# Two stores at the end of a kernel, each issued as two halves on two DMA queues

## The chip, the cores and the metric

The kernel runs on one core of a Trainium2 chip. The core has a matrix engine (TensorE, PE in the profile), VectorE (DVE), ScalarE (ACT), GpSimd (POOL) and SyncE (SP). Transfers between the core's on-chip memory (SBUF) and the device's memory run on 16 DMA engines. An instruction on an engine's own queue issues a transfer; in this kernel SyncE, ScalarE and GpSimd issue them. A store's completion is counted in a semaphore, and the program ends when all stores are complete.

The metric is the device time of one execution, in microseconds (us). Three runs of the kernel before took 293.83, 294.07 and 294.32 us; the median is 294.07.

## What is computed

The input `x` has 8 batches of 1024 tokens with 512 features in float32; `cond` is one row of 512 per batch. Cut to what matters, the reference is:

```
for every batch b:
    ae    = layernorm(cond[b]) * ln_g + ln_b
    h     = gelu(ae @ w1 + b1)
    xw    = h @ w2 + b2                          # two halves, each [512, 8]
    layer = base_layer + x_a @ x_b.T             # a term of rank 8 for every batch
    y     = x + (x + x @ layer)                  # 2x + x @ layer
    ys    = cond[b] / sqrt(512)
    d     = rsqrt((ys*ys) @ (weight*weight) + 1e-8)
    out[b] = y + ((y * ys) @ weight) * d
```

For each batch the two layers fold into one matrix of 512 by 512, so that `out[b] = x[b] @ M[b]`. Making the eight matrices takes the first part of the kernel; multiplying 1024 token rows by each fills the rest. To keep float32 accuracy each operand of a product is split into a rounded part and a remainder, and three matmuls are added up (rounded by rounded, and the two cross terms).

## The kernel before

**The main loop** (`main`) takes batches 0 to 4 and half of batch 5 in tiles of 128 tokens. TensorE accumulates 12 matmuls per tile in PSUM, ScalarE copies the result to SBUF and issues its store on its own queue, 256 KB at a time. SyncE loads `x` in blocks of 512 tokens (1 MB), and the splitting and the making of later matrices run beside it.

**The end of the kernel** is the class `Seven`. For the second half of batch 5 and for batches 6 and 7 it multiplies blocks of 512 tokens by 512 columns with seven products of half size instead of eight, in Strassen's manner. One call of `part` does one such block of 512 tokens. The seven products come in the order of `Seven.ORDER`: 1, 5, 6, 2, 7, 3, 4. Every product has 12 matmuls, six for each of two row groups of 128 tokens (`m` is 0 or 1). The last product of the last part is therefore number 4, and its result is the lower left quarter of the block: 256 tokens by 256 columns.

Output tiles are `o1` (the upper 256 tokens) and `o2` (the lower 256 tokens), each of 128 partitions, two row groups and 512 columns. After a product, ScalarE copies a PSUM bank into a quarter of such a tile, or VectorE adds a bank onto it (line 1032).

**The last call**, `s7.part(1, last=True)` (line 1128), differs in two ways from the others. The bank that products 6, 7 and 4 share is two tiles, one per row group (line 1020), so that the first row group can be copied while TensorE works on the second. And every quarter is stored by itself: the store of products 2, 7 and 3 is issued by SyncE, that of product 4 by ScalarE, row group by row group (lines 1035 and 1036). So after the last matmul of the first row group ScalarE copies it (A, 128 tokens by 256 columns, 128 KB), issues its store, copies the second row group (B, likewise) and issues that store.

**What sets the order.** Matmuls always keep the order in which the program writes them. `ve`, `se` and `sy` are wrappers of VectorE, ScalarE and SyncE; while `InOrder.on` is true, what is issued through them keeps the written order too, and it is set to true before the parts begin (line 1120). So in the stretch around the change every instruction stands on its engine in the order of the code. Waits between engines come from semaphores, which the framework derives from the parts of tiles that are read and written. Stores and loads on SyncE's and ScalarE's queues take eight semaphores in rotation. At the end SyncE waits for all of them, before the engines meet at closing barriers.

Of the kernel before, what the change touches and what calls it, by code (L numbers as in the profile page):

```python
# [14 lines left out]
P = 128  # L15
# [15 lines left out]
def cond_resid_kernel(ctx: ExitStack, tc: tile.TileContext, small, cond, condrows, consts,  # L31
# [32 lines left out]
    ve, se, sy = InOrder(nc.vector), InOrder(nc.scalar), InOrder(nc.sync)  # L64
# [333 lines left out]
    rows = ppool.tile([P, KC, D], F32, tag="ph", name="rows")  # L398
# [506 lines left out]
    class Seven:  # L905
# [99 lines left out]
        def part(self, g, steps=(), last=False, then=None):  # L1005


            b, bank, steps = self.b, {}, iter(steps)
            o1, o2 = (pools["late"].tile([P, 2, D], F32, tag="o2", name=f"o{i}_{b}_{g}", bufs=4)
                      for i in range(2))  # L1010
            for p in self.ORDER:
                key = {5: "z", 3: "z", 2: "v"}.get(p, "w")

                def new(key, count=1):
                    pool, tag = (po, "po") if key == "z" else (acc, "acc")
                    bank[key] = [pool.tile([P, 2, HD], F32, tag=tag, name=f"s{key}{i}_{b}_{g}")
                                 for i in range(count)]

                if p in (1, 5):
                    new(key, 2 if p == 1 and last else 1)  # L1020
                self.product(g, p, bank[key], p in (1, 5))
                if p == 1:
                    new("v")
                o, cols = {1: (None, None), 2: (o1, slice(0, HD)), 3: (o1, slice(HD, D)),
                           6: (o1, slice(HD, D)), 4: (o2, slice(0, HD)), 5: (o2, slice(HD, D)),
                           7: (o2, slice(HD, D))}[p]
                for m, u in enumerate(bank[key]):
                    u, to = (u, slice(0, 2)) if len(bank[key]) == 1 else (u[:, 0:1], slice(m, m + 1))
                    if p == 1:
                        se.copy(bank["v"][0][:, to], u)  # L1030
                    elif p in (3, 7):
                        ve.tensor_add(o[:, to, cols], u, o[:, to, cols])
                    else:
                        se.copy(o[:, to, cols], u)
                    if last and p in (2, 3, 7, 4):
                        self.store(se if p == 4 else sy, o, g, int(p in (4, 7)), to, cols)
                    elif p in (3, 4):
                        self.store(sy, o, g, int(p == 4), to, slice(0, D))
                next(steps, None)
                if p == 7 and then:  # L1040
                    then()

        def store(self, queue, o, g, half, ms, cols):
            at = g * HT + 2 * P * half
            queue.dma_start(
                out[self.b, at + P * ms.start:at + P * ms.stop, cols].rearrange("(m p) d -> p m d", p=P),
                o[:, ms, cols])

    def late_pools():
        making.close()  # L1050
# [147 lines left out]
```

## Time and profile before

| | |
|---|---|
| median of three runs | 294.07 us |
| the profiled execution | 293.74 us |
| its span in the profile | 291.9 us |
| TensorE busy | 286.3 us (98%) |
| VectorE, ScalarE busy | 214.8 us (74%), 175.0 us (60%) |
| granted clock of TensorE | 0.998 on average |
| last PSUM copy by ScalarE (B) | starts 288.52, takes 0.37 us |
| last store issued (B) | at 288.93 us, 0.34 us at the issue |

The profile is of one execution. Busy times are sums over the span; times of instructions count from the span's start. A name such as `ACTq` stands for the queue side of an engine: instructions that issue transfers or handle semaphores, which are not counted as busy. "Landing" is the time from the issue of a transfer to its completion. In a table by stretches the columns are the stretch, its length and TensorE's busy time with its count of instructions, then the same for weight loads, VectorE, ScalarE and GpSimd, then the granted clock, the share of the 16 DMA engines that was busy, and GB/s. Nearly every line shows `L62` or `L45`, the wrappers through which the instructions go; tiles and times tell them apart.

### The profile page before, as it was taken

The page shows a single profiled execution, that of the slowest core. Times are in us where ns is not written, and L with a number is a line of the kernel's source. Part 1 is how long each engine was busy: PE and PEld are TensorE (multiplying, and loading weights), DVE is VectorE, ACT ScalarE, POOL GpSimd, SP SyncE. Part 2 cuts the span into 40 slices and gives each one's busy share as a digit, 9 for nine tenths or more (in the row PEclk, how much of TensorE's full clock was granted, in tenths as well). Part 3 has the DMA queues.
Part 4 walks back from the last instruction along what each step waited for, and adds up shares of the span by engine and source line. Part 5 has one row for each costly group of instructions (what it writes and reads, how often), then busy time and mean ns, then how long its engine had stood idle before and what let it go on. Part 6 is the DMA issues. An engine that isn't in the chain of part 4 may idle for free.

```text
span 291.9 us, 4100 instructions
## 1 busy us (share of the span) xinstructions
PE 286.3 (98%) x1519; PEld 225.2 (77%) x1519; DVE 214.8 (74%) x295; ACT 175.0 (60%) x272; POOL 35.9 (12%) x77
## 2 busy tenths in 40 slices
PE   7999999999999999999999999999999999999995
PEld 3665566467877878888877888887888889999994
DVE  2889898989916999519799565326789977798912
ACT  5757263286849884658654575544658745856641
POOL 2111000202944560000022000000000000000000
PEclk9999999999999999999999999999999999999999
DMA  7999999992799783332328114262175870852334
GB/s 209 405 429 413 411 403 405 390 383 90 187 321 322 235 250 116 110 145 93 159 80 263 55 72 135 83 216 74 72 251 176 291 257 1 290 204 87 142 146 144
DMA packets 19924, 62.14 MB, mean 213 GB/s; under 512 B 2736, under 2 KB 4016, under 8 KB 15552
## 3 DMA queue, kind: packets, MB, share of 16 engines
q1 hardware_dynamic: 9504, 43.76, 40.7%
q10 hardware_dynamic: 6912, 12.32, 11.5%
q0 software_dynamic: 3488, 5.79, 7.5%
q8 instruction: 12, 0.20, 0.3%
q14 instruction: 8, 0.07, 0.1%
HBM read 44.02 MB, written 17.84 MB: 212 GB/s over the span
## 4 chain that ended last, share of the span: by engine, by line
PE 96%; DMA 2%; ACT 0%; DVE 0%; SPq 0%; ACTq 0%; issue 0%
PE po L45 42%; PE pp L45 20%; PE sw L45 9%; PE px L45 5%; PE sz L45 5%; PE pg L45 4%; PE pq L45 4%; PE sv L45 2%; DMA b_raw<-in_baseT 2%; PE pr L45 1%; PE pt_t L45 1%; PE ps_t L45 0%; PE pq_v L45 0%; PE pq_z L45 0%; ACT o L62 0%; DVE o L62 0%
## 5 line engine op out<-in xcount | busy, mean ns | idle before, releaser
L45 PE MATMUL po<-ph,xs 128*128 128x512 f32 x352 | 113.7, 392 | 0.0
L45 PEld LDWEIGHTS po<-ph,xs 128*128 128x128 f32 x352 | 66.0, 188 | 15.6 <-issue 1.7
L45 PE MATMUL po<-pl,xs 128*128 128x512 f32 x176 | 68.6, 390 | 0.0
L62 ACT COPY o<-po 128x512 f32<-128x512 f32 x44 | 25.9, 588 | 35.0 <-PE po L45 35.0
L45 PEld LDWEIGHTS po<-pl,xs 128*128 128x128 f32 x176 | 33.0, 188 | 6.7
L62 DVE TENSOR_TENSOR xs<-x,xs 128x1024 fp32r<-128x1024 f32 (+1 forms) x23 | 27.0, 1176 | 15.0 <-ACT xs L62 15.0
L62 DVE TENSOR_TENSOR nl_p<-n,nh_p 128x1024 fp32r<-128x1024 f32 x21 | 25.7, 1222 | 12.4 <-ACT nh_p L62 12.4
L62 ACT CAST nh_p<-n 128x1024 fp32r<-128x1024 f32 x21 | 22.1, 1054 | 14.6 <-DVE n L62 10.9
L62 ACT CAST xs<-x 128x1024 fp32r<-128x1024 f32 x22 | 23.0, 1056 | 3.6 <-DMA x<-in_x 3.6
L62 ACT COPY q<-pp 128x512 f32<-128x512 f32 x30 | 17.4, 586 | 8.7 <-PE pp L45 8.6
L542 POOL DMA_DIRECT2D fa<-kept_a x28 | 13.8, 508 | 58.3 <-PE pr L45 54.0
L45 PE MATMUL pp<-nh_p,sh 128*128 128x512 f32 x48 | 19.0, 396 | 0.0
L45 PE MATMUL pp<-nh_p,sl 128*128 128x512 f32 x48 | 18.7, 390 | 0.0
L45 PE MATMUL pp<-nl_p,sh 128*128 128x512 f32 x48 | 18.7, 390 | 0.0
L62 DVE SCALAR_TENSOR_TENSOR n<-w_sb,ysT,d 128x512 f32<-128x512 f32 x24 | 16.9, 748 | 0.9 <-DMA d<-d_out 0.9
L62 ACT CAST sh<-sraw 128x1024 fp32r<-128x1024 f32 (+1 forms) x14 | 12.9, 926 | 6.8 <-DVE sraw L62 6.8
L62 DVE TENSOR_TENSOR sl<-sraw,sh 128x1024 fp32r<-128x1024 f32 (+1 forms) x14 | 14.9, 1067 | 2.2 <-ACT sh L62 2.2
L62 DVE TENSOR_TENSOR pl<-q,ph 128x1024 fp32r<-128x1024 f32 (+1 forms) x10 | 11.1, 1116 | 6.9 <-ACT ph L62 6.9
L45 PE MATMUL px<-w,hT 128*32 128x512 f32 x128 | 15.6, 599 | 0.0
L62 ACT COPY o<-sw 128x512 f32<-128x512 f32 (+1 forms) x12 | 6.2, 518 | 15.4 <-PE sw L45 12.3
L62 DVE TENSOR_TENSOR q<-pr,q 128x512 f32<-128x512 f32 x14 | 8.8, 688 | 7.9 <-PE pr L45 7.8
L62 DVE TENSOR_TENSOR n<-n,n 128x1024 f32<-128x1024 f32 x12 | 14.5, 1225 | 0.1
(199 smaller groups left out, 576.6 us busy)
## 6 DMA issues: line engine op xcount, KB each, us to landing
w<-in_w SPq DMA_DIRECT2D x16, 1024.0 KB, 10.4
x<-in_x SPq DMA_DIRECT2D x16, 1024.0 KB, 5.6
out<-o ACTq DMA_DIRECT2D x44, 256.0 KB, 2.3
out<-o SPq DMA_DIRECT2D x8, 512.0 KB, 2.9
fa<-kept_a POOLq DMA_DIRECT2D x28, 64.0 KB, 2.7
ft<-kept_t POOLq DMA_DIRECT2D x28, 64.0 KB, 3.5
d<-d_out POOLq DMA_DIRECT2D x6, 256.0 KB, 7.3
w_sb<-in_w SPq DMA_DIRECT2D x1, 1024.0 KB, 8.5
```

Of the source, the lines that this page charges most:

```text
L45: tc.keep_in_program_order(nc.tensor.matmul(*args, **kw))
L62: return lambda *a, **kw: pin(f(*a, **kw)) if InOrder.on else f(*a, **kw)
L542: nc.gpsimd.dma_start(fold[name, b][32 * c:32 * c + 32, :], kept[name, g][32 * i:32 * i + 32, :])
```

## The change

The store of product 4 in the last call of `part` is issued as two transfers per row group. Rows (partitions) 0 to 63 go by ScalarE's queue, and rows 64 to 127 by SyncE's, in that order in the program. `store` gets an argument for the rows, which is all 128 in every other use. All other stores keep their queue, size and place: products 2, 3 and 7 of the last part still go by SyncE. After A's copy there are now one issue on ScalarE and one on SyncE, and the same after B's copy; the bytes stored are the same.

```diff
-                    if last and p in (2, 3, 7, 4):
-                        self.store(se if p == 4 else sy, o, g, int(p in (4, 7)), to, cols)
+                    if last and p == 4:
+                        for queue, rows in ((se, slice(0, P // 2)), (sy, slice(P // 2, P))):
+                            self.store(queue, o, g, 1, to, cols, rows)
+                    elif last and p in (2, 3, 7):
+                        self.store(sy, o, g, int(p == 7), to, cols)
                     elif p in (3, 4):
                         self.store(sy, o, g, int(p == 4), to, slice(0, D))
...
-        def store(self, queue, o, g, half, ms, cols):
+        def store(self, queue, o, g, half, ms, cols, rows=slice(0, P)):
             at = g * HT + 2 * P * half
             queue.dma_start(
-                out[self.b, at + P * ms.start:at + P * ms.stop, cols].rearrange("(m p) d -> p m d", p=P),
-                o[:, ms, cols])
+                out[self.b, at + P * ms.start:at + P * ms.stop, cols].rearrange(
+                    "(m p) d -> p m d", p=P)[rows],
+                o[rows, ms, cols])
```

## The prediction

> **What bounds the kernel now.** I read the page first (engines, queues, the chain that ended last), then the end of the chain in order of time, the instructions of ScalarE and SyncE in the last microseconds, and the DMA engines' share in short stretches there.
>
> From the page, the engines' busy time and the chain by engine:
>
> ```profile
> PE 286.3 (98%) x1519; PEld 225.2 (77%) x1519; DVE 214.8 (74%) x295; ACT 175.0 (60%) x272; POOL 35.9 (12%) x77
> ...
> PE 96%; DMA 2%; ACT 0%; DVE 0%; SPq 0%; ACTq 0%; issue 0%
> ```
>
> TensorE carries the kernel, and the change touches none of its work. It can only act on what follows the last matmul. The end of the chain (start us, us, what):
>
> ```profile
> 286.97 0.70 DVE o L62
> 287.67 0.02 issue
> 287.69 0.38 ACT o L62
> 288.07 0.02 issue
> 288.09 0.34 ACTq L62
> 288.43 0.04 issue
> 288.47 0.02 ACTq L62
> 288.48 0.04 issue
> 288.52 0.37 ACT o L62
> ```
>
> ScalarE copies the first 128 token rows of product 4 out of PSUM (I call them A), issues their store, copies the second 128 rows (B) and issues theirs. The instructions show both issues, and SyncE's last one (the store of product 3):
>
> ```profile
> 288.09 0.34 ACTq L62 DMA_DIRECT2D out<-o  x1
> 288.52 0.37 ACT L62 COPY o<-sw 128x256 f32<-128x256 f32 x1 [0.46 <-PE sw L45]
> 288.93 0.34 ACTq L62 DMA_DIRECT2D out<-o  x1
> ...
> 287.69 0.38 SPq L62 DMA_DIRECT2D out<-o  x1
> ```
>
> Then the DMA engines in stretches (the last two columns are DMA share and GB/s):
>
> ```profile
> 288.00:288.50 0.50, 0.36 (x4) 0.16 (x2) 0.00 (x0) 0.06 (x1) 0.00 (x0) 1.00 0.00 0
> 288.50:289.00 0.50, 0.00 (x0) 0.00 (x0) 0.00 (x0) 0.37 (x1) 0.00 (x0) 1.00 0.80 270
> 289.00:289.30 0.30, 0.00 (x0) 0.00 (x0) 0.00 (x0) 0.00 (x0) 0.00 (x0) 1.00 1.05 352
> 289.30:289.70 0.40, 0.00 (x0) 0.00 (x0) 0.00 (x0) 0.00 (x0) 0.00 (x0) 1.00 1.04 336
> 289.70:289.80 0.10, 0.00 (x0) 0.00 (x0) 0.00 (x0) 0.00 (x0) 0.00 (x0) 1.00 0.62 205
> 289.80:290.20 0.40, 0.00 (x0) 0.00 (x0) 0.00 (x0) 0.00 (x0) 0.00 (x0) 1.00 0.92 312
> 290.20:290.40 0.20, 0.00 (x0) 0.00 (x0) 0.00 (x0) 0.00 (x0) 0.00 (x0) 1.00 0.08 21
> 290.40:291.90 1.50, 0.00 (x0) 0.00 (x0) 0.00 (x0) 0.00 (x0) 0.00 (x0) 0.62 0.00 0
> ```
>
> All 16 engines are full from 288.6 to 290.2 but for a dip at 289.7. Packet by packet the trace has product 3's 256 KB until 289.42, A's 128 KB from 289.32 to 289.77, and B's from 289.77 to 290.3. B's first packet comes 0.85 us after its issue, as product 3's does (287.69 to 288.55). So B starts when its issue allows, just as A's packets run out: issue delay and full engines meet there. B's last completion is recorded at 290.65, 1.73 us after its issue; another 1.28 us of closing waits and barriers end the span. The profiled execution took 293.74 us for a span of 291.93, 0.33 below the median of the three runs, 294.07; I work out the difference in its trace and add it to the median.
>
> **The change part by part.**
>
> ScalarE's issues: two before, two after, for half the rows. The 44 stores of 256 KB in the main loop took 338 to 351 ns each at the issue and these two of 128 KB 338, so length does not show in it; I take 338 again, 0. The other end: A's issue holds ScalarE until 288.43, and B's matmuls had released the copy at 288.38, so it starts some 0.145 late. An issue that shrank could win that much; one that grew to the longest such row on ScalarE, 414 ns at the start beside another queue's issue, would cost 2 x 0.08 = 0.15. What is queued behind A's issue is only B's copy and B's issue.
>
> SyncE's issues: two are added, at 344 to 345 ns by its own 128 KB stores at 285.31 and 286.05. A's half waits for the copy that ends at 288.06 and for SyncE itself, busy with product 3's issue until 288.07; with a wait on an older store's semaphore (17 ns, 0.05 to start) it goes out near 288.18. That is 0.09 behind ScalarE's half, and hidden: the engines are full with product 3 until 289.42, and 288.18 + 0.85 is 289.03. If that cover were gone, 0.09 would show. B's half waits for the second copy, whose end is signalled at 288.90; SyncE answered VectorE's signal of 287.668 at 287.685, so 288.92, level with ScalarE's 288.93. The old signals it also waits for are stores that landed by 281.8. Behind it on SyncE stand only the closing waits, which wait until 290.2 anyway. POOL's queue issues nothing in this stretch. Together 0.
>
> The data: each store still moves 128 packets of 1 KB, 8 per engine at 48 ns, 0.39 us. No row has stores of 64 rows or two queues that issue halves of one tile, so I bound it. Gain: a 256 KB store alone landed after 2.02 us, the 128 KB one after 1.73, so 128 KB less is 0.29 and 64 KB less 0.15, if the halves did not share engines; a share of 0.92 to 1.04 speaks against that. Loss: where the end of one 512 KB store met the start of the next (279.5 to 279.7), 2 KB packets took up to 131 ns instead of 85, a factor of 1.5; on the 16 packets per engine of A and B that is 16 x 48 x 0.5 = 0.39. I take 0, since queues seem to share engines without loss: A on ScalarE's queue followed product 3 on SyncE's at full rate. A store on ScalarE's queue also simply takes its turn behind SyncE's transfer. An x load issued at 178.07 and a store at 178.70 landed together (KB, us to landing), while a store with nothing before it took 2.0:
>
> ```profile
> x<-in_x SPq DMA_DIRECT2D x1, 1024.0 KB, 5.3
> out<-o ACTq DMA_DIRECT2D x1, 256.0 KB, 5.3
> ...
> out<-o ACTq DMA_DIRECT2D x1, 256.0 KB, 2.0
> ```
>
> The Trainium skill speaks against the change on "DMA: Bandwidth & Descriptors", section "Rules for kernel authors": two transfers of disjoint partition halves share the same 16 engines, and one transfer of 128 partitions is to be preferred. By it the data's term is 0 at best. A second page goes further: "SBUF — State Buffer", section "Door 1: The DMA port swizzle", says that partitions 0 to 63 reach 8 of the 16 ports; with the 27.2 GB/s per port that it works with, a half served by itself would run at 218 GB/s, and by my estimate from that page A and B would end 0.43 later. No row of the trace shows a half.
>
> Completions: every store ends with one 4-byte packet on each engine, 9 ns. Two more stores add 2 x 9 ns, 0.02 us.
>
> The closing waits: SyncE goes through the eight semaphores of the stores one after the other, each 0.061 us after the last (290.67, 290.73, ... 291.04). The stores take these eight in rotation; B has the second in that order, so six waits, long satisfied, are still gone through after B has landed. With two more stores in the rotation, A takes the first and second and B the third and fourth; four are left. That is 2 x 0.061 = 0.12 less. Its other end is 0, if the rotation restarts or the order changes.
>
> Sum: 0 + 0 + 0 + 0.02 - 0.12 = -0.10 us; 293.64 against the profiled 293.74, and 293.97 as a median. A kernel like this tells about 0.2%, 0.59 us, from no change, so I forecast no change.
>
> **The rivals.**
>
> The halves slow the packets. For it: nothing here has shown the engines serving half the rows. Against: equal bytes in equal packets. At the factor of 1.5 it gives -0.10 + 0.39, 294.36, still no change. If packets took twice as long, 16 x 48 = 0.77 more, 294.74. It decides from 0.69 us of loss on, that is 91 ns per packet.
>
> A wait takes the place of the copy's freedom (the other side). Four transfers now read two parts of one tile, on two queues. If the row halves made the dependency tracking take A's stores for readers of what the B copy writes, that copy would wait for A's landing: from 288.52 to 290.24 = 1.72 later, 294.07 + 1.72 - 0.10 = 295.69. It decides at once, since any wait on a store's landing is over 0.59. Against it: before, the B copy starts 0.43 us after A's issue, without waiting for its landing, and so did VectorE's second addition at 285.60, 0.29 us after the store of the first (landed 1.97 us after issue); both differ in columns of the tile that stay disjoint.
>
> The halves really help. Overlapping transfers (-0.15) and a shorter issue on ScalarE (-0.145) with the closing waits (-0.12): -0.42 at best, 293.65, still no change; it decides only if more of the landing time went away. Against: full engines, and an issue that was the same for 256 and 128 KB.
>
> The change does nothing at all (rotation not as I read it): +0.02, 294.09.
>
> **How the numbers follow.** The forecast, with or without the closing waits' 0.12: 0.60, of it 0.57 within 0.2%, 0.01 faster and 0.02 slower. Slower packets: 0.18, of it 0.07 within and 0.11 slower, because the price is unmeasured and the doubled one is past the bound. The wait on A's landing: 0.07, slower. The halves help: 0.11, of it 0.06 within and 0.05 faster, since the 0.35 from the last packet to the last completion may shrink too. Something unseen: 0.02 faster, 0.02 slower. Sum: faster 0.08, same 0.70, slower 0.22. The range takes the gain's end with the spread of the runs below the median, 293.65 - 0.15, about 293.5, and above the doubled packets' 294.74 and 0.15 for the spread, 294.9. It leaves out the wait on a landing. The likeliest case's own range is 293.7 to 294.3.
>
> **What would show it.** Right: four issues after 288, two on each queue, B's two level within 0.05; packets of 1 KB still near 48 ns; the last completion within 0.1 of 1.73 after issue; four satisfied waits after it instead of six, the time from the last landing to the span's end near 1.16 instead of 1.28. Wrong: packets over 60 ns or a DMA share of 1 that reaches past 290.4; a gap before the B copy; ScalarE's issue clearly off 338 ns; SyncE's half of B out after 289.

## The result and the profile after

The changed kernel took 294.57 us (median of 11 runs, 294.31 to 294.87), the kernel before 293.86 (11 runs, 293.75 to 294.32). The two medians are 0.71 us apart. The ratio that was recorded from the fast runs is 1.0019 with a 95% interval of 1.0012 to 1.0027: slower by 0.56 us, 0.35 to 0.79. The profiled execution has a span of 292.53 us against 291.93, 0.60 more. So it is a small loss. It is just under the 0.59 us that I had called the limit of what a measurement of this kernel tells, but the interval excludes no change.

TensorE's row is what it was, and so is the chain by engine:

```profile
PE 286.4 (98%) x1519; PEld 225.3 (77%) x1519; DVE 214.8 (73%) x295; ACT 175.0 (60%) x272; POOL 36.4 (12%) x77
...
PE 96%; DMA 1%; ACT 0%; DVE 0%; ACTq 0%; SPq 0%; issue 0%
```

The loss stands in the end of the chain (start us, us, what):

```profile
287.65 0.38 ACT o L62
288.03 0.02 issue
288.05 0.56 ACTq L62
288.61 0.04 issue
288.65 0.02 ACTq L62
288.67 0.04 issue
288.71 0.37 ACT o L62
```

The issue of A's first half holds ScalarE for 0.56 us; before, the issue of all of A took 0.34. The copy of B starts at 288.71, although TensorE had finished B's matmuls at 288.34. The second pair of issues, as the instructions of ScalarE and the rows of the stores show them (duration min/median/max in ns, then first and last start):

```profile
288.71 0.37 ACT L62 COPY o<-sw 128x256 f32<-128x256 f32 x1 [0.69 <-PE sw L45]
289.11 0.50 ACTq L62 DMA_DIRECT2D out<-o  x1
...
L62 SPq DMA_DIRECT2D out<-o x1: 467/467/467, 289.1 to 289.1; - x1
L62 ACTq DMA_DIRECT2D out<-o x1: 498/498/498, 289.1 to 289.1; - x1
```

Both queues issue B's halves at the same moment, as the change means them to, but each for 0.47 to 0.50 us. What the DMA engines did (last two columns: share of the engines, GB/s):

```profile
289.70:289.90 0.20, 0.00 (x0) 0.00 (x0) 0.00 (x0) 0.00 (x0) 0.00 (x0) 1.00 0.78 190
289.90:290.20 0.30, 0.00 (x0) 0.00 (x0) 0.00 (x0) 0.00 (x0) 0.00 (x0) 1.00 0.03 7
290.20:290.50 0.30, 0.00 (x0) 0.00 (x0) 0.00 (x0) 0.00 (x0) 0.00 (x0) 1.00 0.75 178
290.50:290.90 0.40, 0.00 (x0) 0.00 (x0) 0.00 (x0) 0.00 (x0) 0.00 (x0) 0.52 0.76 192
```

Two things are new. From 289.9 to 290.2 the engines are all but idle (a share of 0.03), where before B's packets followed A's. And after it they move 178 to 192 GB/s instead of 312. Packet by packet SyncE's half of B runs from 290.23 to 290.68 and ScalarE's half from 290.52 to 290.95: one after the other with some overlap, in 1 KB packets of 61 to 68 ns on average instead of 48. The time from issue to landing of B's store before, and of B's two halves after (shortest, median, longest):

```profile
DMA to landing us min/median/max: 1.7/1.7/1.7
```

```profile
DMA to landing us min/median/max: 1.9/2.1/2.2
```

From TensorE's signal that B is done, the way to the end can be added up without what happened earlier in each execution. I call this the tail. It comes from the trace's records of instructions and semaphores in one execution of each kernel, in us:

| part of the tail | before | after | difference |
|---|---|---|---|
| signal to the start of B's copy | 0.145 | 0.365 | +0.220 |
| B's copy, and on to the last issue | 0.402 | 0.401 | 0 |
| that issue to the last completion | 1.728 | 2.208 | +0.480 |
| last completion to the end | 1.281 | 1.216 | -0.065 |
| tail | 3.556 | 4.190 | +0.634 |

TensorE was 0.036 earlier in the second execution, which gives the 0.60 between the spans. Within the +0.480, ScalarE's half of B has its first packet 1.41 us after its issue instead of 0.85 (+0.56); its packets take 0.43 instead of 0.53 (-0.10); the completion after them is the same within 0.02. SyncE's half, issued 4 ns earlier, has its first packet after 1.12. So 0.27 is a later start that both halves have, and 0.29 is how much later the second half starts than the first; I call this the second half's turn.

### The profile page after: what moved, and what is told of

The parts are those of the page before. It is cut to its first block, busy times and chain, and to the rows that moved or that the text cites. A ratio compares the mean times of both kernels' runs of the same rounds, so it can differ in the third digit from the quotient of the medians.

```text
span 292.5 us, 4105 instructions
## 1 busy us (share of the span) xinstructions
PE 286.4 (98%) x1519; PEld 225.3 (77%) x1519; DVE 214.8 (73%) x295; ACT 175.0 (60%) x272; POOL 36.4 (12%) x77
## 4 chain that ended last, share of the span: by engine, by line
PE 96%; DMA 1%; ACT 0%; DVE 0%; ACTq 0%; SPq 0%; issue 0%
PE po L45 42%; PE pp L45 20%; PE sw L45 9%; PE px L45 5%; PE sz L45 5%; PE pg L45 4%; PE pq L45 4%; PE sv L45 2%; DMA b_raw<-in_baseT 1%; PE pr L45 1%; PE pt_t L45 1%; PE ps_t L45 0%; PE pq_v L45 0%; PE pq_z L45 0%; ACT o L62 0%; DVE o L62 0%
```

## The experiments

The question was what made the issues long and the data late. Theory I: the two queues share a path for their issues and disturb one another. Theory II: a store of 64 rows is slow by itself. Each ratio below is to the kernel before on the same chip, with a 95% interval; the runs were made on several chips. Each tail and each time at the end of the kernel is of one profiled execution. What an edit leaves alone repeats well in them: B's copy and the step to the last issue take 0.401 to 0.404 us in every run but the one with all halves on one queue. The edits shown are to the changed kernel, but for those of the ladder and of the last group, which are to the kernel before.

**Both halves on one queue.**

```diff
-                        for queue, rows in ((se, slice(0, P // 2)), (sy, slice(P // 2, P))):
+                        for queue, rows in ((se, slice(0, P // 2)), (se, slice(P // 2, P))):
```

> Both halves of each store go by ScalarE's queue, one after the other. Theory I, two queues that issue at the same time share one path for their issues (in the changed kernel 0.47 to 0.56 us each instead of 0.34, and the later half's data 0.3 us late): alone on one queue each issue is back at 0.34 us; the second copy is held by one more issue of 0.34, the last issue comes near 289.6 and lands some 1.65 later, about 291.3 against 290.65: +0.5 us with two closing waits fewer. Theory II, a store of 64 rows is slow in itself: issues of 0.5 us or more even without a neighbour, the copy held by 0.5 more, +0.9 us or more. On the packets both agree with the changed kernel if a half alone is slow for its rows: 1 KB packets of 62 to 75 ns in place of 48.

Measured 295.51 us against 293.98, ratio 1.0054 (1.0041 to 1.0066); tail 5.13, +1.58. ScalarE at the end:

```profile
288.07 1.19 ACTq L62 DMA_DIRECT2D out<-o  x2
289.36 0.37 ACT L62 COPY o<-sw 128x256 f32<-128x256 f32 x1 [1.32 <-PE sw L45]
289.76 1.12 ACTq L62 DMA_DIRECT2D out<-o  x2
```

With no neighbour on another queue the issues take 0.54, 0.61, 0.47 and 0.61 us. Theory I as the cause of the long issues falls. The packets take 62 to 66 ns, also without a neighbour: each half's packets end before the next half's begin.

**Two queues, split by columns.**

```diff
-                        for queue, rows in ((se, slice(0, P // 2)), (sy, slice(P // 2, P))):
-                            self.store(queue, o, g, 1, to, cols, rows)
+                        for queue, part in ((se, slice(0, P)), (sy, slice(P, HD))):
+                            self.store(queue, o, g, 1, to, part)
```

> The same two queues at the same time, but split by columns: all 128 rows by 128 columns each, packets of 512 bytes. Theory I (shared issue path): issues of 0.47 to 0.56 us and a second half that starts 0.3 us late remain, so the last landing is 2.1 us or more after its issue and the kernel +0.4 to +0.7 us. Theory II (64 rows): issues back near 0.34, first packet 0.85 after the issue, landing near 1.73, and the kernel between -0.1 and +0.1 us.

Measured 294.22 us, ratio 1.0009 (0.9997 to 1.0021); tail 3.70, +0.14. Here two issues of 128 rows overlap on two queues:

```profile
289.57 0.37 ACT L62 COPY o<-sw 128x256 f32<-128x256 f32 x1 [0.49 <-PE sw L45]
289.98 0.36 ACTq L62 DMA_DIRECT2D out<-o  x1
```

The four issues take 0.33 to 0.42 us, so theory I keeps at most 0.08 per issue. The longest, 0.42 on SyncE, is no neighbour's doing: an issue of 128 rows that follows product 3's by 0.09 us takes 0.42 there also while ScalarE issues nothing (in the run below with A whole on SyncE). B's first piece lands after 1.74, as a whole store does, and the second after 1.91. The second piece lands 0.17 after the first, a cost of splitting that has nothing to do with 64 rows. Its packets start 0.13 after the first piece's, less than half of the 0.29 between the two halves of 64 rows.

**Even and odd rows.**

```diff
-                        for queue, rows in ((se, slice(0, P // 2)), (sy, slice(P // 2, P))):
+                        for queue, rows in ((se, slice(0, P, 2)), (sy, slice(1, P, 2))):
```

> Two queues, 64 rows each, but even rows by ScalarE and odd rows by SyncE, so that each half reaches over the whole tile. If the slow packets of the changed kernel (62 to 75 ns instead of 48) come from 64 neighbouring rows, they are back near 48 ns and a half takes 0.2 us instead of 0.35 to 0.4; if they come from two queues or from small stores, they stay. Theory I expects the issues to stay at 0.47 to 0.56 us either way, the second copy 0.2 late, and the kernel at +0.3 to +0.5 us; theory II with the rows' place as its cause expects -0.1 to +0.2.

Measured 294.72 us, ratio 1.0028 (1.0017 to 1.0039); tail 4.16, +0.60. The packets are back at 47 to 49 ns, so it is the 64 neighbouring rows that slow them. It buys almost nothing: the last half lands 2.15 us after its issue instead of 2.21, and the tail is 0.03 shorter than the changed kernel's. The second half still starts 0.28 after the first, though the first is now served at the normal pace, so the slow packets don't make that turn. The issues stay at 0.47 to 0.58 us: they don't depend on which 64 rows it is.

**Only B in halves, and only A in halves.**

```diff
+                        halves = ((se, slice(0, P // 2)), (sy, slice(P // 2, P)))
-                        for queue, rows in ((se, slice(0, P // 2)), (sy, slice(P // 2, P))):
+                        for queue, rows in halves if m == 1 else ((se, slice(0, P)),):
```

> Only the second store (B) as two halves, the first whole by ScalarE as before. The second copy should start as before, 0.145 us after its matmuls (not 0.37). B's halves should still land 1.9 and 2.2 us after their issue instead of 1.73. Both theories: +0.48 for the landing and -0.06 to -0.12 for the closing waits, +0.4 us; if the held copy were the whole cost, +0.0.

> Only the first store (A) as two halves, the second whole by ScalarE as before. By the runs so far a 64-row store holds its engine 0.54 to 0.61 us at the issue instead of 0.34, on one queue or two: the second copy should start 0.22 us later than before against its matmuls, the last store should land 1.73 after its issue as before, and one closing wait fewer gives 0.06 back: +0.16 us. If instead the two queues' halves of A delayed B's data too (a theory that the engines or the issue path stay clogged), the last landing would be over 1.9 us after its issue and the kernel +0.35 or more.

(The second has `m == 0` for `m == 1`.) With only B in halves: 294.56 us, ratio 1.0023 (1.0011 to 1.0036), tail +0.55; the copy starts 0.146 after the signal, as before, and the last half lands after 2.28. With only A in halves: 294.20 us, ratio 1.0008 (0.9999 to 1.0016), tail +0.17; the copy starts 0.362 after the signal, and the whole B lands after 1.75. ScalarE of the two, B alone and A alone:

```profile
288.38 0.34 ACTq L62 DMA_DIRECT2D out<-o  x1
288.82 0.37 ACT L62 COPY o<-sw 128x256 f32<-128x256 f32 x1 [0.47 <-PE sw L45]
289.22 0.58 ACTq L62 DMA_DIRECT2D out<-o  x1
```

```profile
288.33 0.56 ACTq L62 DMA_DIRECT2D out<-o  x1
288.98 0.37 ACT L62 COPY o<-sw 128x256 f32<-128x256 f32 x1 [0.68 <-PE sw L45]
289.38 0.34 ACTq L62 DMA_DIRECT2D out<-o  x1
```

The two parts of the loss come apart: A's halves cost the held copy, B's halves the landing, and in the tails 0.17 and 0.55 add up to 0.72 against 0.63 together. Most of the difference is B's landing: 2.28 where B alone is in halves, 2.21 where A's halves went before. In the times only B's part is clear of no change; A's 0.17 is read from its profile.

**One half alone.**

```diff
-                        for queue, rows in ((se, slice(0, P // 2)), (sy, slice(P // 2, P))):
-                            self.store(queue, o, g, 1, to, cols, rows)
+                        self.store(se, o, g, 1, to, cols, slice(0, P // 2) if m == 1 else slice(0, P))
```

> Rows 64 to 127 of the second store are left out altogether, so a single 64-row store stands alone at the end; that part of the output is not written. If the half is slow in itself: issue near 0.55 us, first packet 1.1 us after it, packets of 62 to 67 ns, landing 1.9 to 2.0 us after the issue although it has half the bytes. If it was the neighbour that slowed it: issue 0.34, first packet 0.85 and landing near 1.5 us. The difference to 2.2 us, the later half's landing in the changed kernel, is the price of the second half's turn.

```profile
289.31 0.37 ACT L62 COPY o<-sw 128x256 f32<-128x256 f32 x1 [0.47 <-PE sw L45]
289.71 0.54 ACTq L62 DMA_DIRECT2D out<-o  x1
```

The lone half has an issue of 0.54 us, its first packet 1.20 after it, packets of 66 ns, and lands 1.99 us after its issue. Half the bytes land 0.26 later than the whole store (1.73). The other 0.22 of the +0.48 comes with the second half. One execution, read from its profile only.

**A ladder of row counts.** In the main loop, on ScalarE's queue, some of the 256 KB stores are cut into pieces; the first edit has 64+64, 32+96, 16+112, 8+120, 48+80 and 32+32+32+32 rows, the second the taller piece first.

```diff
-        nc.scalar.dma_start(out[b, t * P:(t + 1) * P, :], o)
+        ends = {1: (80, P), 2: (96, P), 3: (112, P), 4: (64, P), 5: (32, 96, P)}.get(t, (P,))
+        for lo, hi in zip((0,) + ends, ends):
+            nc.scalar.dma_start(out[b, t * P + lo:t * P + hi, :], o[lo:hi, :])
```

> Stores of other row counts, all by ScalarE's queue in the main loop: of every eight tiles, one in two pieces each of 64+64, 32+96, 16+112, 8+120 and 48+80 rows, one in four of 32, two whole. Theory 128 (a full height of 128 rows is the quick case and everything below costs the same): issues of 0.5 to 0.6 us at every other count. Theory count (the issue grows as rows get fewer): 96 and 112 rows near 0.4, 32 and 16 rows over 0.6. Theory powers: 64, 32, 16 and 8 alike and quicker than 48, 80, 96, 112, 120.

> The ladder again in the main loop on ScalarE's queue, with the taller piece first, away from any issue just ahead of it: 80+48, 96+32, 112+16, 64+64 rows, and 32+64+32, where 64 rows stand in the middle. Theory 64 (just this count is slow): first pieces of 80, 96 and 112 rows take 0.32 to 0.36 us at the issue, 64 rows 0.47 or more, and 64 in second place 0.6 while 48, 32 and 16 in second place take 0.43. Theory tall: issues grow with the rows below 128, so 80, 96 and 112 take 0.45 us or more in first place.

Both kernels are longer (303.99 and 299.84 us, one execution each); only single stores are read from them. Three stores of the second ladder, of 64, of 112 and of 128 rows in that order, each with no issue just ahead of it:

```profile
L905 ACTq DMA_DIRECT2D out<-o x1: 486/486/486, 159.4 to 159.4; - x1
```

```profile
L905 ACTq DMA_DIRECT2D out<-o x1: 323/323/323, 155.9 to 155.9; - x1
```

```profile
L905 ACTq DMA_DIRECT2D out<-o x1: 357/357/357, 173.9 to 173.9; - x1
```

From both ladders, typical values in us (rows of 2 KB). "First packet" counts from the start of the issue, where the DMA engines were idle until then. The landings are of pieces with no other tile's transfer under way; a shorter piece's own second piece follows close behind it.

| rows | issue, none ahead | issue, right behind one | first packet, none ahead | landing, none ahead |
|---|---|---|---|---|
| 8 | 0.29 | 0.34 (one) | 0.76 (one) | not read |
| 16 | 0.32 | 0.45 | 0.82 to 0.83 | 1.57 |
| 32 | 0.32 | 0.44 | 0.82 to 0.84 | 1.62 |
| 48 | 0.33 | 0.44 | 0.82 to 0.83 | 1.93 |
| 64 | 0.47 to 0.51 | 0.61 | 1.16 (two) | 2.2 to 2.3 |
| 80 | 0.34 | 0.44 | 0.85 (one) | 2.0 |
| 96 | 0.32 | 0.43 | 0.83 to 0.84 | 2.2 |
| 112 | 0.32 | 0.44 | 0.82 to 0.83 | 2.25 |
| 120 | 0.34 (one) | 0.34 | not read | not read |
| 128 | 0.34 to 0.36 | not seen | 0.84 to 0.87 | 2.03 |

Of the counts tried, 64 alone has the long issue, by about 0.16 us in both columns, and all three theories of the first ladder fall. 64 alone has the late first packet, too, by about 0.3 us: from the end of the issue the first packet takes 0.66 us, where every other count that could be read takes 0.48 to 0.52. This is the later start that both halves have in the changed kernel. The first 64-row issue on a queue in a run takes longer still, 0.54 to 0.58 in every run with such stores; a later one with none ahead 0.47 to 0.51. A's halves are the first, so by my estimate from the 0.56 and 0.50 of ScalarE's two issues, some 0.06 of the 0.22 belongs to that. 32 rows issued behind a middle piece of 64 took 0.59 where the same piece behind 32 took 0.44, so part of the price falls on the next issue. Why just 64, the traces don't say. In landing 64 is not so alone: 96 and 112 rows also took longer than 128, with a first packet at the usual time.

**Pieces of other heights in the changed kernel.**

```diff
-                        for queue, rows in ((se, slice(0, P // 2)), (sy, slice(P // 2, P))):
+                        for queue, rows in ((se, slice(0, 32)), (sy, slice(32, P))):
```

> Each store as two pieces on two queues as in the changed kernel, but rows 0 to 31 by ScalarE and 32 to 127 by SyncE. The ladder had issues of 0.32 us for 32 rows, 0.33 for 48, 0.36 for 128 and 0.47 to 0.49 for 64, each 0.12 more directly behind another issue. Theory 64 (just 64 rows are the slow case): ScalarE's issues near 0.32, the second copy 0.15 after its matmuls or less, as before, the last landing 1.75 to 1.95 after its issue: 0.0 to +0.2 us. Theory pieces (any split on two queues costs what the halves cost): +0.5 us or more.

> The same with rows 0 to 47 by ScalarE and 48 to 127 by SyncE. Theory 64: ScalarE's issues near 0.33 and SyncE's at 0.33 to 0.44, no longer hold of the second copy, the last landing 1.75 to 2.0 after its issue: 0.0 to +0.25 us. Theory pieces: +0.5 us or more.

The first one's last two stores:

```profile
L62 SPq DMA_DIRECT2D out<-o x1: 327/327/327, 289.7 to 289.7; - x1
L62 ACTq DMA_DIRECT2D out<-o x1: 366/366/366, 289.7 to 289.7; - x1
```

With 32+96 rows: 294.23 us, ratio 1.0010 (0.9999 to 1.0021), tail +0.26. With 48+80: 294.31 us, ratio 1.0007 (0.9999 to 1.0016), tail +0.41. The issues are short in both (0.32 to 0.42), and the copy starts 0.193 after the signal, 0.05 more than before instead of 0.22. The hold is thus the 64 rows' own. The landings are 2.01 and 2.22, more than theory 64 had allowed, with issues of normal length. Late data is therefore not only a matter of the issue. The packets separate it in part: the second piece starts 0.14 and 0.11 after the first; the last piece's packets end 1.51 and 1.73 us after its issue instead of 1.38; and from there to the last completion it takes 0.50 and 0.49 us instead of 0.35. Why uneven pieces complete so late, the traces don't say.

With the columns, there are now three pairs on two queues without 64 rows, and their second pieces start 0.11 to 0.14 after the first. The three pairs of B's halves with 64 rows have 0.28 to 0.29. So some 0.15 of the second half's turn is also seen only with 64 rows. It starts while the first half's packets still run (290.52 against 290.68 in the changed kernel). What orders the two is not shown.

**Whole stores, and the closing waits.** The first edit sends A whole by SyncE and B whole by ScalarE. The second leaves the end as it was and issues six earlier stores in two pieces of 128 rows each, so that the last store gets another place in the rotation of semaphores. The third, shown here, does both.

```diff
-                        self.store(se if p == 4 else sy, o, g, int(p in (4, 7)), to, cols)
+                        self.store(se if p == 4 and m == 1 else sy, o, g, int(p in (4, 7)), to, cols)
                     elif p in (3, 4):
-                        self.store(sy, o, g, int(p == 4), to, slice(0, D))
+                        for i in ((slice(0, 1), slice(1, 2)) if self.b >= NB - 2 else (to,)):
+                            self.store(sy, o, g, int(p == 4), i, slice(0, D))
```

> No halves: the first store (A) whole by SyncE, the second (B) whole by ScalarE. The second copy no longer waits for an issue on ScalarE: it should start 0.04 us after its matmuls instead of 0.145, and B's issue come 0.1 earlier. A's packets, behind those of product 3, end no earlier, so B's data can gain at most those 0.1: -0.1 to 0.0 us. If two whole stores on two queues cost anything by themselves, +0.2 or more.

> No halves; the end is as before. Six earlier stores of 512 KB (products 3 and 4 of the three parts before the last) are issued as two of 256 KB each, one per row group, so that six more stores take their turn in the rotation of eight semaphores and the last store has the last one that SyncE looks at. If the satisfied closing waits cost 0.061 us each, six of them go: 1.28 us from the last landing to the end becomes 0.91, and the kernel -0.37 us. If they cost nothing on the way to the end, 0.0; if the extra issues get in the way of loads, slower.

> The rotation as in the run with six earlier stores issued in two, and the first store (A) whole by SyncE, the second (B) whole by ScalarE. If the closing waits count, -0.37 us for them and 0.0 to -0.05 for the copy that no longer waits for an issue: 293.6 beside 294.0. This would be under both kernels.

Apart: 293.93 us against 293.99, ratio 1.0004 (0.9992 to 1.0016); tail -0.05. The copy starts 0.022 after the signal, and B lands after 1.80 instead of 1.73: its first packet comes 0.90 after its issue instead of 0.85, while A's packets still run. Rotation: 293.73 us against 293.94, ratio 0.9995 (0.9983 to 1.0007); tail -0.375, of it -0.369 from the last completion to the end (0.912 instead of 1.281). Both: 293.53 us, ratio 0.9989 (0.9978 to 1.0001), tail 3.13, -0.42:

```profile
287.77 0.37 ACT L62 COPY o<-sw 128x256 f32<-128x256 f32 x1 [2.96 <-DVE o L62]
288.49 0.37 ACT L62 COPY o<-sw 128x256 f32<-128x256 f32 x1 [0.34 <-PE sw L45]
288.89 0.34 ACTq L62 DMA_DIRECT2D out<-o  x1
```

By the 0.369 us for six of them, each satisfied closing wait costs 0.0615 us. The last version has the shortest tail and the lowest median of all, but its interval still touches 1, so that it beats the kernel before is shown in the profile and not in the times.

## Why the prediction was wrong

I forecast no change, 293.97 us, with a chance of 0.70 for less than 0.2% either way. The kernel is slower by 0.19%, with an interval that excludes no change. The time lies in the range, 293.5 to 294.9, and the direction was missed. That the range holds it is luck: its upper end was made for packets that take twice as long, and the loss came another way. All four signs that I had listed for being wrong were seen (slow packets, a gap before B's copy, a long issue on ScalarE, SyncE's half of B out after 289). By steps:

- **ScalarE's issues, taken as 0.** This step failed. I argued that length does not show in an issue, since 256 KB and 128 KB took the same; but the edit changed the number of rows, not only the bytes, and no row of the profile had 64. The issue took 0.56 us instead of 0.34, beyond the longest row I had bounded it with (0.41). It holds the second copy by 0.22 us more, and A's halves alone cost 0.17 in the tail. The step named rightly what stands behind A's issue: B's copy.
- **SyncE's issues, taken as 0.** Their place was right: A's half went out at 288.12, close to the 288.18 of the forecast, and B's at 289.104, level with ScalarE's 289.108. Their length was not (0.55 and 0.47 instead of 0.34).
- **The data, taken as 0, at most +0.39.** This step failed, too, and is the larger term: the last landing came 0.48 later after its issue. I had bounded it by the packets' pace. The packets did slow, by the factor of 1.3 to 1.4 that the rival had set at 1.5, but the even and odd rows restored their pace and shortened the tail by 0.03 only. The loss lay before the first packet: 0.27 from the half's own later start, which the ladder finds with 64 rows alone, and 0.29 from the second half's turn; packets that end sooner give 0.10 back. I had counted B's 0.85 us from issue to first packet as fixed, and never put a price on a change of it.
- **The completions, +0.02.** The time from the last packet to the last completion is longer by 0.02 in one execution, but this shows nothing: with as many stores it took 0.42 us instead of 0.37 in the run with even and odd rows.
- **The closing waits, -0.12.** The mechanism was right: six earlier stores more in the rotation took away 0.369 of the 0.37 expected. In the changed kernel it gave 0.065, since ScalarE's half, with the third semaphore, lands last and not SyncE's with the fourth.
- **The rivals.** "The halves slow the packets" had the right sign and the wrong cause. "A wait takes the place of the copy's freedom" did not happen: the copy starts at 288.71, while A's first half lands at 290.07. "The halves really help" counted on a shorter issue; it became longer.
- **Readings of the profile before.** Three were a little off, and no term of the sum hangs on them. Product 3's first packet is at 288.58, 0.90 us after its issue and not 0.85. The store of 178.70 landed 0.69 us after the load, not together with it, which fits taking its turn all the same. A copy that no issue holds still starts 0.022 after the signal, so an issue that shrank could have won 0.12 and not 0.145.

On the two rules that I had weighed: the Trainium skill, "DMA: Bandwidth & Descriptors", section "Rules for kernel authors", says that transfers of disjoint partition halves serialize. The two halves of B start 0.29 apart and overlap for 0.16 us, so here they do so in part. The same page, section "Issuing engines are not separate DMA queues", says that a second issuing engine only saves the time of issuing. The runs agree: the same halves on one queue have a tail of 5.13 us instead of 4.19, and the long issues come with 64 rows on one queue as on two. The port rule of "SBUF — State Buffer", section "Door 1: The DMA port swizzle", agrees with slow packets for neighbouring rows (61 to 68 ns) and normal ones for even and odd rows (47 to 49). My estimate of 0.43 us from that page was far over what the pace cost, 0.06 us in the landing and 0.03 in the tail.

## What to carry to other kernels

A store at the very end is paid by its latency, so price an edit there from issue to first packet and to completion, not by bytes and engine pace; a shape that the profile doesn't contain has no price yet, and a ladder of shapes in a quiet part of the kernel gives it cheaply. Cutting the last transfer in two added an issue and a turn for the second piece here, and with 64 rows a longer issue and a later first packet besides. What follows the last landing can be worth more than the store: the place of the last store in the order of the closing waits moved 0.37 us here.

## What the hardware showed that I had not expected

- A store of 64 rows typically holds its queue 0.47 to 0.61 us at the issue, on ScalarE's and on SyncE's queue, whichever 64 rows; 16, 32, 48, 80, 96, 112 and 128 rows take 0.32 to 0.36 with no issue just ahead. The reason is open.
- With the DMA engines idle, the first packet of a 64-row store came 1.16 us after the start of its issue; with 16 to 128 rows of the other counts it came after 0.82 to 0.87. The reason is open here, too.
- The first 64-row issue on a queue took 0.54 to 0.58 us, a later one with none ahead 0.47 to 0.51.
- An issue directly behind another on the same queue took about 0.12 us longer (32 rows: 0.44 instead of 0.32).
- Packets of 1 KB read from 64 neighbouring rows took 61 to 68 ns instead of 48, also with only one such store under way (66 ns); from every second row of the tile, 47 to 49.
